# Ordering the start of a convolution-attention kernel by a list schedule, loading one image once, and projecting d and u onto repeated columns

## The chip, the cores and the metric

The kernel runs on one core of a Trainium2 chip. The metric is the device time of one execution in microseconds (us). Every time named here comes from an execution that fell in the fast state, except that single runs of a kernel have the state "unknown", which is said where it matters. Two sessions of the same kernel differ by 1 to 2 us; so a time is compared with the kernel before from the same rounds.

## The reference, cut to what matters

A tensor of four images, 64 x 64 tokens of 96 channels, goes through two layers. In the first, each image is normalised by groups and by tokens and projected to 288 + 3 x 1536 columns. A linear recurrence over the 4096 tokens with 16 states a channel follows:

```python
xn = (x - mu) * jax.lax.rsqrt(var + EPS) * ln_gamma + ln_beta
proj = xn.reshape(B, L, C) @ W_in + b_in
value, gate, delta = proj[..., :C], jax.nn.sigmoid(proj[..., C:2*C]), proj[..., 2*C:3*C]   # u, g, d
# A, Bm, Cm: the other 3 * C * S columns, S = 16
def step(h, ins):
    A_t, B_t, C_t, d_t, u_t, g_t = ins
    d = d_t[..., None]
    h_new = d * (A_t * h) + d * (B_t * u_t[..., None])
    y = g_t * jnp.sum(C_t * h_new, axis=-1)
    return (h_new, y)
# x = x + scan(...) @ W_out + b_out; then linear attention and a feed-forward block with rounding to 8 bits
```

## The kernel before: the parts that the change and the argument touch

The work is cut into 32 chunks of 512 tokens (eight for each image), and each chunk into twelve tiles of 128 partitions, which are 32 channels times 4 of the 16 states. A loop over 384 steps has one tile's scan on VectorE in each step; B and A are projected three and one steps ahead, and the small work of other chunks is hung on steps. Before the loop a straight sequence prepares chunk 0. A float32 product is computed as three products of split operands: `xs` holds 96 high rows and 32 low rows, `xl` the other low rows twice.

```python
    for i in range(NCH):
        load_gx(0, i, "x")            # image 0 in wide rows, for the group statistics alone
    ...
    load_x(0, 0)                      # and again in the order of the chunks
    raw0 = load_raw("cha", 0, A0)
    raws = [load_raw("chb", B0, C * S)]
    load_x(0, 1)
    raws += [load_raw("chb", c0, C * S) for c0 in (A0, C0)]
    ...
        def low(self):
            ...
            nc.vector.tensor_tensor(lo, self.ps, xs[0:C, :].bitcast(F32), ALU.subtract)
            nc.sync.dma_start(xl[0:64, :].bitcast(F32), lo[0:64, :].bitcast(F32))
            nc.sync.dma_start(xl[64:P, :].bitcast(F32), lo[0:64, :].bitcast(F32))
            nc.sync.dma_start(xs[C:P, :].bitcast(F32), lo[64:C, :].bitcast(F32))
    ...
        def copy(self, k, cg, engine):        # d or u of 32 channels onto four groups of partitions

            t = rep[self.b, self.i][:, k, cg]
            for q in range(4):
                engine.dma_start(
                    t[q * 32 : (q + 1) * 32], self.dd[cg * 32 : (cg + 1) * 32, k]
                )
    ...
    first.proj(2)
    first.d_out()
    first.copy(0, 0, nc.sync)
    low(2, 0, nc.vector)
    first.proj(0)
    first.du_out()
    first.copy(1, 0, nc.scalar)
    first.proj(1)
    first.gate_out()
    low(2, 1, nc.vector)
    low(2, 2, nc.vector)
    for cg in (1, 2):
        first.copy(0, cg, nc.sync)
        first.copy(1, cg, nc.sync)
```

The loop, which stays as it is:

```python
    while s < K or any(n >= s for n in steps):
        # B of tile s+3 (TensorE, ACT), A of s+1, C of s (TensorE), u*B of s+2 (GpSimd)
        ...
        if 0 <= s < K:
            tiles[s].scan()           # VectorE
        if 0 <= s + 1 < K:
            tiles[s + 1].a_mul()      # VectorE
        if 0 <= s < K and not tiles[s].on_pool:
            tiles[s].c_mul()          # VectorE
        call(s)                       # whatever hangs on this step
```

## Time and profile before

| | before |
|---|---|
| median of the first 4 runs | 1274.65 us (1273.69 to 1275.44) |
| first scan, fourth scan (step 3) | 46.2, 57.7 us |
| scan of step 12 (second chunk) | 92.1 us |
| VectorE busy, whole run | 88% |

A row of the timeline reads: start in us, duration, engine, line of the kernel, operation, output<-inputs; in brackets the idle time of the engine just before and what ended it. `SPq` is SyncE's queue of DMA issues. A row of stretches reads: stretch, length, then for TensorE, its weight loads, VectorE (DVE), ScalarE (ACT) and GpSimd (POOL) the busy time and the number of instructions, then the granted clock of TensorE (1.00 is full speed), the busy share of the DMA engines and GB/s. The lines of the kernel before stand in the prediction below.

### The profile page before, as it was taken

The numbers are of one execution on the slowest core, as the hardware profiler recorded it, in microseconds if no ns is written. First come the engines' busy times: TensorE is split into PE (matmuls) and PEld (weight loads), VectorE is DVE, ScalarE is ACT, GpSimd is POOL, SyncE is SP. The second block draws the span as 40 slices with busy tenths as digits, with TensorE's granted clock in tenths as the row PEclk, the third lists the DMA queues.
The fourth block names the chain that finished last, engine by engine and source line by source line (L and its number), as shares of the span: only waits on it lengthen the run. The fifth ranks groups of instructions, "written<-read, shape, count | busy, mean of one in ns | idle before, by whom it ended". The sixth has DMA issues, their size and how long they took to land. (4 is left out here: it accounts for less than half of the span.)

```text
span 1273.8 us, 18972 instructions
## 1 busy us (share of the span) xinstructions
PE 1171.9 (92%) x5782; PEld 882.7 (69%) x5782; DVE 1119.6 (88%) x2082; ACT 817.0 (64%) x1825; POOL 1034.8 (81%) x1189
## 2 busy tenths in 40 slices
PE   3789999999999999889999999989999999999684
PEld 2567777777777777667777777657777777777363
DVE  5479999989999999969999999869999999999274
ACT  4355555555555687567777777656676777766664
POOL 4367888888888899869999999869999889979354
PEclk7689999999999999989999999989999999999655
DMA  8567777767777778657677887656777777765221
GB/s 202 118 139 145 159 153 159 165 145 158 154 160 162 154 164 174 141 128 156 149 171 155 170 170 159 136 117 143 167 156 170 162 154 155 157 147 106 69 57 38
DMA packets 102260, 185.99 MB, mean 146 GB/s; under 512 B 42881, under 2 KB 47429, under 8 KB 102158
## 3 DMA queue, kind: packets, MB, share of 16 engines
q1 hardware_dynamic: 87708, 109.78, 37.3%
q0 software_dynamic: 13680, 74.72, 29.6%
q8 instruction: 46, 0.75, 0.3%
q10 hardware_dynamic: 770, 0.28, 0.1%
q14 instruction: 56, 0.46, 0.1%
HBM read 70.69 MB, written 24.77 MB: 75 GB/s over the span
## 5 line engine op out<-in xcount | busy, mean ns | idle before, releaser
L604 POOL TENSOR_TENSOR bu<-bu,rep 128x512 f32<-128x512 f32 x384 | 557.3, 1499 | 44.1 <-DMA rep<-dd 21.8
L601 ACT ACTIVATE bu<-Bps,b_bac 128x512 f32<-128x512 f32 x384 | 264.2, 688 | 305.0 <-PE Bps L241 281.7
L620 DVE TENSOR_TENSOR_SCAN h<-Aps,state,bu 128x512 f32<-128x512 f32 x336 | 426.5, 1269 | 9.5 <-DVE Aps L613 0.5
L613 DVE SCALAR_TENSOR_TENSOR Aps<-Aps,b_bac,rep 128x512 f32<-128x512 f32 x384 | 282.7, 736 | 61.8 <-PE Aps L241 53.0
L241 PE MATMUL Bps<-xs,w 128*128 128x512 f32 x768 | 271.4, 435 | 7.6 <-ACT bu L601 7.5
L241 PE MATMUL Aps<-xs,w 128*128 128x512 f32 x768 | 252.2, 409 | 12.4 <-DVE h L620 11.4
L241 PE MATMUL Cps<-xs,w 128*128 128x512 f32 x768 | 244.8, 400 | 0.0
L653 POOL TENSOR_TENSOR ch<-ch,h 128x512 f32<-128x512 f32 x128 | 193.6, 1512 | 3.0 <-ACT ch L650 2.8
L644 DVE SCALAR_TENSOR_TENSOR ch<-Cps,b_bac,h 128x512 f32<-128x512 f32 x256 | 189.8, 741 | 2.8 <-PE Cps L241 2.7
L241 PEld LDWEIGHTS Aps<-xs,w 128*128 128x128 f32 x768 | 141.2, 192 | 70.3 <-DVE h L620 40.7
L241 PEld LDWEIGHTS Cps<-xs,w 128*128 128x128 f32 x768 | 146.4, 191 | 36.2
L241 PEld LDWEIGHTS Bps<-xs,w 128*128 128x128 f32 x768 | 131.9, 194 | 50.9 <-issue 26.0
L241 PE MATMUL Bps<-xl,w 128*128 128x512 f32 x384 | 154.3, 402 | 0.0
L241 PE MATMUL Aps<-xl,w 128*128 128x512 f32 x384 | 154.3, 402 | 0.0
L241 PE MATMUL Cps<-xl,w 128*128 128x512 f32 x384 | 152.7, 398 | 0.0
L659 POOL DMA_DIRECT2D ch<-ch x95 | 89.4, 942 | 25.4 <-DMA ch<-ch 20.6
L650 ACT ACTIVATE ch<-Cps,b_bac 128x512 f32<-128x512 f32 x128 | 88.0, 688 | 27.3 <-PE Cps L241 26.5
L241 PEld LDWEIGHTS Cps<-xl,w 128*128 128x128 f32 x384 | 73.1, 190 | 18.5
L241 PEld LDWEIGHTS Bps<-xl,w 128*128 128x128 f32 x384 | 73.7, 192 | 17.4
L241 PEld LDWEIGHTS Aps<-xl,w 128*128 128x128 f32 x384 | 73.0, 190 | 17.2
L241 PE MATMUL dug_ps<-xs,w_dug 128*96 128x512 f32 x192 | 62.8, 409 | 10.4 <-DMA xs<-lo 10.4
L620 DVE TENSOR_TENSOR_SCAN h<-Aps,bu 128x512 f32<-128x512 f32 x48 | 58.0, 1209 | 4.8 <-POOL bu L604 3.3
(166 smaller groups left out, 1776.2 us busy)
## 6 DMA issues: line engine op xcount, KB each, us to landing
ch<-ch POOLq DMA_DIRECT2D x95, 768.0 KB, 6.8
rep<-ddd SPq DMA_DIRECT2D x124, 384.0 KB, 7.0
ddd<-dd SPq DMA_DIRECT2D x31, 384.0 KB, 3.1
xl<-lo SPq DMA_DIRECT2D x64, 128.0 KB, 3.1
gx<-in_x_dram SPq DMA_DIRECT2D x32, 192.0 KB, 3.9
x<-in_x_dram SPq DMA_DIRECT2D x32, 192.0 KB, 3.0
xatd<-xat SPq DMA_DIRECT2D x32, 192.0 KB, 3.2
xal<-xatd SPq DMA_DIRECT2D x32, 192.0 KB, 3.1
```

Of the source, the lines that this page charges most:

```text
L241: nc.tensor.matmul(ps, lhsT=wt[:, n], rhs=mv, start=(n == 0), stop=(n == 2))
L601: nc.scalar.activation(self.bu, self.b_ps, AF.Identity, bias=self.bias(0))
L604: nc.gpsimd.tensor_tensor(self.bu, self.bu, rep[self.b, self.i][:, 1, self.cg], ALU.mult)
L613: nc.vector.scalar_tensor_tensor(self.a_ps, self.a_ps, self.bias(1), rep[self.b, self.i][:, 0, self.cg], ALU.add, ALU.mult,)
L620: nc.vector.tensor_tensor_scan(self.h, self.a_ps, self.bu, 0.0 if self.i == 0 else state[self.sh, self.cg], ALU.mult, ALU.add,)
L644: nc.vector.scalar_tensor_tensor(self.slot(), self.c_ps, self.bias(2), self.h, ALU.add, ALU.mult)
L650: nc.scalar.activation(self.ch, self.c_ps, AF.Identity, bias=self.bias(2))
L653: nc.gpsimd.tensor_tensor(self.ch, self.ch, self.h, ALU.mult)
L659: nc.gpsimd.dma_start(chs[g, 0], chs.pop((g, sh)), accum_op=ALU.add)
```

## The change

Its intent is to shorten the time until the loop runs at its pace. It has five parts: image 0 is loaded once, in the chunks' layout; d and u of chunk 0 are projected straight onto 128 partitions by weights whose columns are repeated four times, so that 24 copies go; the low rows of chunk 0 are written in place by three subtractions instead of one and three DMAs; everything up to step 3 is issued in the order of a list schedule (it picks one job after the other, that which can start first, by the author's costs and landing times); and matmuls without use ("fillers") fill TensorE's planned gaps to hold its clock. Core of the diff:

```diff
     for i in range(NCH):
-        load_gx(0, i, "x")
+        load_x(0, i)
+        gxt[0, i] = xt[0, i]
# ... the second loads of x(0, 0) and x(0, 1) and the argument "tag" go
+    def repeat(n):
+        for k, c0 in enumerate((2 * C, 0)):
+            for cg in range(NCG):
+                c = c0 + cg * 32
+                nc.gpsimd.tensor_copy(
+                    w_rep[:, n, k * NCG + cg].rearrange("p (q c) -> p q c", q=4),
+                    w_dug[:, n, c : c + 32].unsqueeze(1).to_broadcast([P, 4, 32]),
+                )
# ... weights are now copied per group of 32 channels (512 columns); the bias rows get a second set for d and u
+    class Plan:
+        HOP = 0.15
+        LOOK = 0.3
# ... job(engine, cost, fn, after=, take=, free=, late=); run() picks the job that can start first,
# ... among those within LOOK that of the lower rank, then that of the longer tail
+                e = j["engine"]
+                if fill is not None and e == "PE":
+                    for _ in range(int(max(0.0, t - self.time.get(e, t) - 0.2) / 0.3)):
+                        fill()
+                j["fn"](*j["args"])
+                j["end"] = self.time[e] = t + j["cost"]
# ... group norm: diagonal, spread and its copy in two halves for image 0; for images 1 to 3:
-        for n, name in enumerate(("moments", "mean", "root", "diagonal", "spread")):
+        for n, name in enumerate(("moments", "mean", "root", "diagonal", "spread", "spread_out")):
+        def low_in_place(self, n):
+            if n == 0:
+                split[self.b, self.i] = self.xs, sb("xl", [P, TC], F32R, f"xl_{self.nm}")
+            xs, xl = split[self.b, self.i]
+            dst, c0, c1 = ((xs[C:P], 64, C), (xl[0:64], 0, 64), (xl[64:P], 0, 64))[n]
+            nc.vector.tensor_tensor(dst, self.ps[c0:c1], xs[c0:c1].bitcast(F32), ALU.subtract)
+
+        def wide(self, k, cg):
+
+            ps = self.wd[k, cg] = bank("M", [P, TC], f"wide{k}{cg}_ps")
+            project(ps, w_rep[:, :, k * NCG + cg], split[self.b, self.i])
+
+        def wide_d(self, cg):
+            if cg == 0:
+                rep[self.b, self.i] = sb("rep", [P, 2, NCG, TC], F32, f"rep_{self.nm}")
+            nc.scalar.activation(
+                rep[self.b, self.i][:, 0, cg], self.wd[0, cg], AF.Identity,
+                bias=b_rep[:, 0, cg : cg + 1],
+            )
+
+        def wide_du(self, cg):
+            t = rep[self.b, self.i]
+            nc.vector.scalar_tensor_tensor(
+                t[:, 1, cg], self.wd[1, cg], b_rep[:, 1, cg : cg + 1], t[:, 0, cg],
+                ALU.add, ALU.mult,
+            )
# ... planned_start(): one job for each operation
+        raw = [land(f"raw{n}", t) for n, t in enumerate((13.0, 16.5, 20.0))]
+        for n in range(3):
+            a = job("DVE", 0.7, first.low_in_place, n, after=[a], free=["M:x"] if n == 2 else [])
+        d, u = [], []
+        for cg in range(NCG):
+            t = mm(0.7, first.wide, 0, cg, after=[a, w["rep"]], key=f"M:d{cg}")
+            d.append(job("ACT", 0.69, first.wide_d, cg, after=[t, b, *d[-1:]], free=[f"M:d{cg}"]))
+            t = mm(0.7, first.wide, 1, cg, after=[t], key=f"M:u{cg}")
+            u.append(job("DVE", 0.74, first.wide_du, cg, after=[t, d[-1]], free=[f"M:u{cg}"]))
# ... the tiles up to step 3; then rank 1: the second chunk
+        job("DVE", 0.7, second.low, after=[a], free=["M:x2"])
# ... the filling matmul
+            nc.tensor.matmul(
+                awake[0][:, 0:P], lhsT=ident, rhs=ident, start=True, stop=True
+            )
```

## The prediction

> **What bounds the kernel now.** I read the busy shares and the forty slices of the page, then the busy time of the engines in stretches, then the timeline of the first 95 us with its waits. The slices first (busy tenths, one digit for 31.8 us):
>
> ```profile
> PE   3789999999999999889999999989999999999684
> ...
> DVE  5479999989999999969999999869999999999274
> ```
>
> After the third slice VectorE is at nine tenths and more for nearly the whole run: about 32.4 us for each chunk of twelve tiles (twelve scans, twelve multiplications of A, eight of C, and the small work). The change touches none of that; it orders only what comes before step 3 of the loop. So its worth is read from the first slices. Busy time in stretches of the start (columns: stretch, its length, PE, weight loads, DVE, ACT, POOL, granted clock, DMA share, GB/s):
>
> ```profile
> 0.00:26.00 26.00, 9.22 (x46) 6.58 (x46) 13.11 (x35) 10.72 (x18) 12.09 (x32) 0.77 0.83 209
> 26.00:46.00 20.00, 11.69 (x29) 7.67 (x30) 7.93 (x15) 9.58 (x15) 4.20 (x5) 0.59 0.67 141
> 46.00:58.00 12.00, 8.33 (x29) 6.11 (x28) 7.52 (x10) 2.92 (x6) 5.29 (x5) 0.78 0.54 128
> 58.00:92.00 34.00, 29.16 (x115) 22.34 (x113) 22.77 (x34) 17.90 (x45) 22.87 (x22) 0.84 0.59 129
> 92.00:124.60 32.60, 31.84 (x144) 23.81 (x143) 32.15 (x54) 17.65 (x44) 25.76 (x28) 1.00 0.67 137
> ```
>
> From 26 to 46 us no engine is busy for even 60%. Something is waited for there, and the waits say what (timeline of GpSimd, then of VectorE and TensorE; start, duration, instruction, idle before it and what ended that):
>
> ```profile
> 41.80 1.27 POOL L604 TENSOR_TENSOR bu<-bu,rep 128x512 f32<-128x512 f32 x1 [12.12 <-DMA rep<-dd]
> 47.65 1.29 POOL L604 TENSOR_TENSOR bu<-bu,rep 128x512 f32<-128x512 f32 x1 [4.58 <-DMA rep<-dd]
> 54.00 3.72 POOL L604 TENSOR_TENSOR bu<-bu,rep 128x512 f32<-128x512 f32 x3 [5.06 <-DMA rep<-dd]
> ```
> ```profile
> 46.21 1.21 DVE L620 TENSOR_TENSOR_SCAN h<-Aps,bu 128x512 f32<-128x512 f32 x1
> ...
> 57.74 1.21 DVE L620 TENSOR_TENSOR_SCAN h<-Aps,bu 128x512 f32<-128x512 f32 x1
> 61.48 0.76 DVE L613 SCALAR_TENSOR_TENSOR Aps<-Aps,b_bac,rep 128x512 f32<-128x512 f32 x1 [2.53 <-PE Aps L241]
> ```
> ```profile
> 56.44 1.17 PE L241 MATMUL dug_ps<-xs,w_dug 128*96 128x512 f32 x2 [3.67 <-DMA xs<-lo]
> ```
>
> GpSimd waits 21.8 us in three waits for the copies of d and u, which are 24 DMAs of 64 KB; SyncE issues them at about 0.6 us each (16 in 13.75 us). The first scan begins at 46.21, the fourth (step 3) at 57.74. The same SyncE queue holds back the transfers of the second chunk's low rows, so that TensorE stands until 56.44. These two times, 57.74 and 56.44, are what the change has to move.
>
> **What the Trainium skill says.** "TensorE: Matmul & The Clock Gate", What's actually happening: after an idle window of some 3.4 us the array falls to half rate and needs about as long of work to come back. The trace agrees: the granted clock is 0.50 from 15 to 30 us, and a matmul of 512 columns takes about 0.43 us there against 0.235 after 48 us. "DMA: Bandwidth & Descriptors", Specifications: the line rate needs 512 bytes or more. The trace agrees: while loads of x in rows of 384 bytes ran alone (522 packets at 12.5 to 14.5 us), most slices showed 115 to 200 GB/s; the 1,536-byte loads of gx ran at 279 from 2 to 6 us. "SBUF — State Buffer", SBUF: two separate sides: VectorE with two SBUF inputs and GpSimd lock each other out. The trace is consistent: the power of 128x4 took 1.65 us beside the weight subtractions and 1.04 us at 67.9 us.
>
> **The change part by part.**
>
> *x once.* The eight gx loads (3.5 us to landing, rows of 1,536 bytes) become x loads with rows of 384 bytes. At 165 to 190 GB/s (estimate from the slices above) 0.197 MB takes 1.03 to 1.2 us, eight take 8.3 to 9.5 us against about 7. From the first bytes at 1.9 us the last lands near 10.9 instead of 9.3: +1.6 us on the statistics. Two separate x loads (2.2 us of DMA) go, so the weights land when they did.
>
> *Chain to the first projection*, before: last group statistics end 10.7, normalised z 22.65, low rows 25.58, after three DMAs TensorE starts at 28.86. After, with the same rows of the trace: statistics end 12.3; aggregate, mean and root 3.15 (10.72 to 13.83, as before) gives 15.45; diagonal 0.4, spread of half the columns 0.7 instead of 1.1, copy 0.3: 16.9. Centre now ran earlier, scale 0.56: 17.5. Statistics 1.03, offset 0.1, power 1.05 to 1.65 (say 1.35): 20.0 (the other three GpSimd operations, 1.3 us, leave the path). Apply on VectorE 1.7 (four took 1.69 at 1247 us), last transpose 0.4, affine 0.73, upper 0.58, hops: 23.7. Low rows in place, three subtractions of 0.69: 25.8. TensorE starts there, 3 us earlier; the subtractions cost 1.4 us more of VectorE but no DMA (3.3 us).
>
> *d and u by repeated columns.* Out: d_out, which stood behind three weight casts until 34.11, and 24 copies until 52. In: six projections onto 128 rows instead of two onto 96, 18 matmuls at 0.235 = 4.2 us of TensorE (7.7 if the clock stays low), three ACT copies of 0.69, three VectorE multiplications of 0.74 instead of one. Two GpSimd repetitions (2 x 2.2 us by the author's own figure) and 0.4 MB of DMA lie beside the chain. First multiplication of B: 25.8 + 0.7 + 0.7 + 0.75 = 28.0; with 1.3 us on GpSimd the first scan starts at **29.5 against 46.21: 16.7 us** earlier.
>
> *The list schedule* then has to fit all the rest. VectorE after 25.8: du 3 x 0.74, A 4 x 0.75, scans 3 x 1.22, C 2 x 0.75, about four of the nine weight subtractions at 1.0 (the raw weights land too late for more), second chunk 1.1 + 0.7 = 16.2 us. So step 3 can't start before **42**, 15.7 us earlier. TensorE: 6 + 6 + 4 + 3 projections of 0.7 = 13.3 us, to 39, if the filling matmuls hold the clock. So the 16.7 us are partly lost again: VectorE takes the place of the DMA.
>
> *The second chunk* has rank 1, so its statistics, power 1.8, apply 1.55, transpose 0.5, affine and upper 1.3, low 0.7 fill holes. With VectorE full they come late, I think low rows at 40 to 43. Its three DMAs (3.3 us) follow, and the next matmul in TensorE's order is proj 2 of that chunk: TensorE resumes at 43 to 46 against 56.44, **10.5 to 13.5 us** earlier, and probably at half clock again.
>
> *After step 3* nothing is different: the 4.66 us wait for gx at 80 us and the slow tiles (34 us for nine, against 24 in the steady state) stay.
>
> The sum: between 10.5 and 15.7 us, and I choose 13: 1274.3 - 13.3 = **1261 us**, or 1.0%.
>
> **The rivals.** (1) *VectorE is the only bound and the second chunk gets in early*: then step 3 counts and some of the ten lost microseconds between 58 and 92 go too, since they began with that wait; 17 to 22 us, 1252 to 1257. For it: ACT and GpSimd have room. (2) *Late data in a fixed order*: queues are strict, the plan assumes x at 3.6 + 0.8n and weights at 13.0, 16.5 and 20.0; before, the x rows were slower than that. A cast that waits for its weights ahead of the spread's copy on ACT delays everything by 1 to 3 us, and the clock falls to half if the filling is too thin (up to 12 us of TensorE): only 4 to 8 us, 1266 to 1270. (3) *The start is hidden anyway*: if some later DMA set the pace, nothing would come of it; against it, VectorE is at 97% of the stretch from 92 us on, so an earlier start is an earlier end.
>
> **Range and chances.** The rivals' ends give 1252 to 1269. Faster by over 2% needs 25.5 us, more than the first scan itself gains, so 0.04. Slower by 2% would need a new stall of 39 us in the start: 0.01.
>
> **What would show each step.** First scan near 29.5 and fourth near 42 to 44; no DMA rep<-dd; last x landing near 11; first wide projection near 26; waits of 3 us for xs<-lo in TensorE around 43; granted clock near 1.0 from 26 to 40; the scan that opens the second chunk at about 79 instead of 92.06; the end of the run shifted by the same amount. The prediction is wrong if step 3 starts before 36 (the weight subtractions fitted in earlier), if the wait for xs<-lo is gone, or if the gap between the fourth scan and the second chunk shrinks below 30 us.

## The result, and the profile after

The changed kernel takes **1259.96 us** (median of 4 runs, 1258.66 to 1262.39), before 1274.65. The ratio is **0.9887** with a 95% interval of 0.9869 to 0.9906, so 1.1% less. A ratio is the mean time of one kernel's fast runs over that of the other's of the same rounds, so not quite the ratio of the medians. The prediction said 1261. But the traces show that its sum came out right from parts that did not.

The slices of the changed kernel's page, to be laid beside those of before:

```profile
PE   7989999999999999799999999889999999999683
...
DVE  6779999999999999779999999869999999999275
```

The first two slices are fuller (VectorE 6 and 7 against 5 and 4); from the fourth on they differ by a tenth here and there. The same stretches as in the prediction, now of the changed kernel:

```profile
0.00:26.00 26.00, 18.19 (x107) 16.14 (x107) 14.27 (x35) 9.93 (x15) 14.55 (x41) 0.87 0.83 204
26.00:46.00 20.00, 18.48 (x93) 14.59 (x94) 19.01 (x32) 12.85 (x23) 10.48 (x10) 1.00 0.37 86
46.00:58.00 12.00, 9.42 (x38) 7.00 (x37) 5.36 (x7) 4.68 (x11) 8.29 (x7) 0.86 0.36 90
58.00:92.00 34.00, 28.99 (x116) 21.66 (x115) 26.36 (x38) 17.58 (x45) 22.59 (x22) 0.90 0.71 155
```

From 26 to 46 us VectorE is now busy 19.0 of 20 us, where it was busy 7.9: the wait for DMA has become a full engine. After 46 us it is idle for more than half again. The timeline of the same trace says what each part came to:

```profile
15.75 1.07 ACT L278 CAST w<-raw 128x512 fp32r<-128x512 f32 x1 [2.51 <-DMA raw<-in_L_conv_W_in_dram]
19.43 0.24 ACT L557 COPY gmr<-gmr_ps 128x96 f32<-128x96 f32 x1 [2.61 <-PE gmr_ps L548]
...
35.39 3.25 POOL L742 TENSOR_TENSOR bu<-bu,rep 128x512 f32<-128x512 f32 x2 [5.72 <-DVE rep L666]
...
37.70 1.22 DVE L758 TENSOR_TENSOR_SCAN h<-Aps,bu 128x512 f32<-128x512 f32 x1
```

GpSimd's wait for the copies (12.1 us before) is a wait of 5.7 us for VectorE, and the first scan begins at 37.7 instead of 46.2. It would have been earlier, had the spread of the group statistics not waited for TensorE until 19.4. TensorE's timeline shows why, and what stands at step 4:

```profile
13.98 5.04 PE L1141 MATMUL awake<-ident 128*128 128x128 f32 x22
18.81 0.58 PE L548 MATMUL gmr_ps<-gdg,ones 96*128 96x96 f32 x2
...
48.97 0.70 PE L245 MATMUL dug_ps<-xs,w_dug 128*96 128x512 f32 x2 [2.37 <-DMA xs<-lo]
```

The 11 filling matmuls (listed as 22 instructions, 0.23 us each at half clock) stand in the queue ahead of the spread, whose operand was ready at 13.25. And TensorE still waits for the second chunk's low rows, until 48.97 instead of 56.44. VectorE pays for it (its timeline):

```profile
47.30 1.22 DVE L758 TENSOR_TENSOR_SCAN h<-Aps,bu 128x512 f32<-128x512 f32 x1
53.70 0.76 DVE L751 SCALAR_TENSOR_TENSOR Aps<-Aps,b_bac,rep 128x512 f32<-128x512 f32 x1 [5.18 <-PE Aps L245]
54.56 1.22 DVE L758 TENSOR_TENSOR_SCAN h<-Aps,bu 128x512 f32<-128x512 f32 x1
```

So the gain is 8.5 us at the first scan, 10.4 at the fourth, 7.8 at the fifth and 8.2 at step 12 (83.9). The end of this trace is 13.1 us earlier. Some 5 us came where the change seemed to do nothing.

### The profile page after: what moved, and what is told of

The parts are those of the page before. It is cut to its first block, busy times and chain, and to the rows that moved or that the text cites. A ratio compares the mean times of both kernels' runs of the same rounds, so it can differ in the third digit from the quotient of the medians.

```text
span 1260.7 us, 19196 instructions
## 1 busy us (share of the span) xinstructions
PE 1175.9 (93%) x5885; PEld 890.3 (71%) x5885; DVE 1124.9 (89%) x2093; ACT 818.4 (65%) x1824; POOL 1038.9 (82%) x1198
## 5 line engine op out<-in xcount | busy, mean ns | idle before, releaser
L758 DVE TENSOR_TENSOR_SCAN h<-Aps,state,bu 128x512 f32<-128x512 f32 x336 | 426.7, 1270 | 9.2
L245 PE MATMUL dug_ps<-xs,w_dug 128*96 128x512 f32 x188 | 59.4, 397 | 2.4 <-DMA xs<-lo 2.4
L768 ACT COPY state<-h 128x1 f32<-128x1 f32 x336 | 61.0, 181 | 0.0
```

The source lines that it names most:

```text
L245: nc.tensor.matmul(ps, lhsT=wt[:, n], rhs=mv, start=(n == 0), stop=(n == 2))
L758: nc.vector.tensor_tensor_scan(self.h, self.a_ps, self.bu, 0.0 if self.i == 0 else state[self.sh, self.cg], ALU.mult, ALU.add,)
L768: nc.scalar.copy(st, self.h[:, TC - 1 : TC])
```

## The experiments

Twelve runs followed: nine altered kernels, the changed kernel once more and the kernel before twice. All results were correct. Scans are numbered from 0: s0 is the first, s12 opens the second chunk, s383 is the last. Each timeline number is of one trace; "end" is from s383 to the end of the trace.

| run | median us | ratio to before (95%) | s0 | s3 | s4 | s12 | s12 to s383 | end |
|---|---|---|---|---|---|---|---|---|
| before, first trace | 1274.65 | 1 | 46.2 | 57.7 | 62.4 | 92.1 | 1085.2 | 96.5 |
| before, second trace | 1273.49, one run | | 47.1 | 58.3 | 62.5 | 91.8 | 1084.8 | 95.2 |
| before, third trace | 1268.05, one run | | 46.8 | 58.1 | 62.0 | 90.8 | 1084.5 | 91.0 |
| changed, first trace | 1259.96 | 0.9887 (0.9869-0.9906) | 37.7 | 47.3 | 54.6 | 83.9 | 1082.0 | 94.8 |
| changed, again | 1259.24 | 0.9889 (0.9867-0.9910) | 37.0 | 46.7 | 53.9 | 83.1 | 1079.0 | 94.5 |
| no fillers ahead of the spread | 1258.06 | 0.9881 (0.9858-0.9905) | 35.0 | 44.6 | 50.3 | 79.1 | 1081.3 | 94.9 |
| no fillers at all | 1257.98 | 0.9894 (0.9874-0.9913) | 36.3 | 45.8 | 51.6 | 80.5 | 1081.2 | 95.2 |
| x twice | 1258.05 | 0.9892 (0.9873-0.9912) | 36.6 | 46.2 | 52.8 | 81.4 | 1080.6 | 94.7 |
| low rows by DMA | 1256.39 | 0.9875 (0.9853-0.9897) | 37.1 | 47.0 | 49.7 | 78.6 | 1081.5 | 96.0 |
| copies of d and u | 1268.08 | 0.9963 (0.9952-0.9974) | 39.5 | 58.5 | 61.2 | 89.6 | 1081.3 | 94.9 |
| second chunk in place | 1251.85 | 0.9841 (0.9815-0.9868) | 37.4 | 47.4 | 49.9 | 77.9 | 1081.5 | 90.2 |
| third piece at step 14 | 1253.55 | 0.9851 (0.9827-0.9876) | 36.9 | 46.5 | 52.1 | 74.0 | 1081.6 | 94.8 |
| three edits together | 1250.01 | 0.9820 (0.9793-0.9847) | 35.3 | 45.3 | 47.9 | 69.7 | 1082.3 | 95.5 |
| spread and copy in one step | 1260.55 | 0.9912 (0.9886-0.9937) | 36.0 | 45.6 | 52.4 | 81.1 | 1081.4 | 95.0 |

My theory after the first trace was that the start sets the end, by way of three waits: the fillers, the second chunk's DMA, and a later load that the change leaves alone. The rival was that VectorE, now full, makes these waits worthless.

**The changed kernel again** (no edit).

> The changed kernel once more, unaltered. In its first trace the opening scan of the second chunk (step 12) lay only 8.2 us earlier than before (83.9 against 92.1), while the end lay 13.1 us earlier; the other 5 us appeared at four places far behind the change. Theory 'start only': those 5 us are chance of the two traces, step 12 is again near 84, and the stretch from step 12 to the last scan differs from the first trace's 1082.0 us by up to 2 us. Rival 'something later is better as well': the stretch is again about 1082 us, and 3 us shorter than before's 1085.2 us in every trace.

Step 12 is again near 83, but the stretch after it is 1079.0: neither branch quite, and 3 us between two traces of one program. It is taken up below.

**No fillers ahead of the spread.**

```diff
-                if fill is not None and e == "PE":
+                if fill is not None and e == "PE" and j["fn"].__name__ != "spread":
```

> The 11 filling matmuls ahead of the first spread are left out, the other 32 stay. Theory 'fillers hold the chain': in the changed kernel they run from 14.0 to 19.0 us on TensorE, the spread behind them in the queue starts at 18.8 although its operand was there at 13.3. Without them the first spread is done by 14.5; its copy on ACT then stands behind the first weight cast, which ends at 16.8, so the copy moves from 19.4 to 16.9 and the first scan from 37.7 to 35.2 (2.5 us earlier), the end by 1 to 2.5 us. Rival 'fillers pay': the clock falls lower (it is 0.5 there anyway) and the first projections run at half rate; no gain or a loss of 1 to 3 us.

The timeline of ACT in this run, then of its VectorE:

```profile
14.60 1.06 ACT L278 CAST w<-raw 128x512 fp32r<-128x512 f32 x1 [1.70 <-DMA raw<-in_L_conv_W_in_dram]
15.56 0.23 ACT L557 COPY gmr<-gmr_ps 128x96 f32<-128x96 f32 x1
```
```profile
16.63 1.82 DVE L596 TENSOR_TENSOR z<-x,gmr 128x384 f32<-128x384 f32 x1
18.37 1.76 DVE L235 TENSOR_TENSOR w<-raw,w 128x512 fp32r<-128x512 f32 x1
20.05 0.55 DVE L599 TENSOR_TENSOR z<-z,gmr 128x384 f32<-128x384 f32 x1
```

As expected, the copy now stands behind the weight cast, at 15.56 instead of 19.43, and the first scan is at 35.0, 2.0 to 2.7 us earlier than in the two traces of the changed kernel. Step 12 is 4 to 5 us earlier. The time moved by 1.2 to 1.9 us (medians), inside the intervals: the hold is shown, its worth at the end is not resolved. The lines of VectorE show what holds the chain next: the copy of the second half ends at 17.15 (near the predicted 16.9), but the scale ends at 20.60, because a long centring and a weight subtraction stand before it in VectorE's queue.

**No fillers at all.**

```diff
-        plan.run(stay_awake)
+        plan.run()
```

> No filling matmul at all (43 are left out). Theory 'the later fillers pay': the spread is early as in the run without the first eleven, but the clock is 0.5 until some 5 us after the first projection, projections take 1.28 instead of 0.70 us; first scan 37 to 38.5 instead of 35.0, the end 1 to 3 us later than with the later 32. Rival 'the clock is irrelevant here, VectorE sets the pace': first scan 35 to 36 and the same time as that run.

Stretches of this run, then of the run before it, which keeps 33 fillers (the column after GpSimd's is the granted clock):

```profile
20.00:30.00 10.00, 3.09 (x8) 1.81 (x9) 9.72 (x32) 8.16 (x12) 4.70 (x5) 0.50 0.82 193
30.00:40.00 10.00, 10.00 (x39) 7.97 (x38) 9.04 (x11) 4.22 (x7) 4.12 (x3) 0.85 0.41 94
```
```profile
20.00:30.00 10.00, 8.65 (x61) 7.59 (x61) 9.82 (x33) 7.91 (x12) 4.74 (x5) 0.95 0.74 182
30.00:40.00 10.00, 9.98 (x46) 7.72 (x45) 9.69 (x13) 4.86 (x10) 5.04 (x4) 1.00 0.40 93
```

(The traces of the changed kernel list 88 filling instructions, two for each filler: 44 fillers, and 33 without the first 11. The expectations count one less.) The 33 later fillers do hold the clock, 0.95 against 0.50, and that is worth 1.3 us at the first scan and 1.4 at step 12, less than expected. These are single traces, and two traces of the changed kernel differ there by 0.7 and 0.8. At the end nothing is seen (1257.98 and 1258.06). All 44 together cost at the first scan more than they brought: it comes at 36.3 without them, at 37.0 and 37.7 with them. At the end that is not resolved (ratios 0.9894 and 0.9889).

**x loaded twice**: the loads of before were put back.

> One part undone: image 0 is loaded twice again, eight times in wide rows for the statistics, and x of each chunk by itself. Theory 'loading once is worth nothing here': last statistics end near 10.7 instead of 11.7, but the weights land about 2 us later; the first spread is held by the fillers to 19 anyway; first scan 37 to 39, the end the same within 1.5 us. Rival 'the saved loads pay later': the six x loads that return to the first chunks delay the other transfers there, the stretch from step 12 to the last scan grows from 1079-1082 towards the 1085 of before.

Loading once is worth nothing that shows: 1258.05 against 1259.24, with step 12 1.7 us earlier. The stretch after step 12 is 1080.6, so the rival is out.

**Low rows of chunk 0 by DMA again.**

```diff
-        for n in range(3):
-            a = job("DVE", 0.7, first.low_in_place, n, after=[a], free=["M:x"] if n == 2 else [])
+            if n == 0:
+                a = job("DVE", 0.7, first.low, after=[a], free=["M:x"], late=3.3)
```

(The `for` line stays in the source; only its first turn now does anything.)

> One part undone: the low rows of the first chunk go by one subtraction and three DMAs again, as before the change. Theory 'in place saves the transfer': three subtractions took 2.1 us on VectorE, one and a transfer of 3.3 us take 4.0; first scan at 39 instead of 37.0, step 12 at 84.5 to 85 instead of 83.1, the end later by 1 to 2 us. Rival 'VectorE is the bound in this stretch': it gets 1.4 us back, so the fourth scan stays near 46.7 and the time is the same.

The theory missed: s0 did not move. The rival's numbers hold (s3 at 47.0, the time inside the intervals), but neither foresaw that s4 came 4 to 5 us **earlier**. The second chunk explains it. Its low rows on VectorE, and the issue of their DMA, in this run's timeline:

```profile
32.33 0.69 DVE L623 TENSOR_TENSOR lo<-xnt_ps,xs 96x512 fp32r<-96x512 f32 x1
...
36.76 0.55 SPq L624 DMA_DIRECT2D xl<-lo  x1
```

The same two in the changed kernel:

```profile
44.75 0.68 DVE L623 TENSOR_TENSOR lo<-xnt_ps,xs 96x512 fp32r<-96x512 f32 x1
...
45.46 0.46 SPq L624 DMA_DIRECT2D xl<-lo  x1
```

The order of issue has changed. My reading, which no run shows by itself: while the engines wait for the transfer, the list schedule has a hole, and the second chunk, which has the lower rank, is put into it; in place, the hole closed and the second chunk was pushed back by 12 us. TensorE waits 0.8 us for the first chunk's xs<-lo here and not at all for the second chunk's.

**Second chunk's low rows in place as well.**

```diff
-        job("DVE", 0.7, second.low, after=[a], free=["M:x2"])
+        for n in range(3):
+            a = job("DVE", 0.7, second.low_in_place, n, after=[a], free=["M:x2"] if n == 2 else [])
```

> The low rows of the second chunk too are written in place by three subtractions on VectorE, without the three DMAs. Theory 'the second chunk's DMA sets step 4': TensorE stood 2.4 us until 48.97 for them, its clock fell to half, and the fifth scan was at 54.6; now TensorE goes on at about 47 with its clock at full, the fifth scan comes at 50 to 51, and the end moves by 3 to 4 us. Rival 'VectorE is the bound there': it gets 1.4 us more work, the fifth scan moves by 1 us or less and the time is the same.

The timeline of TensorE and VectorE in this run:

```profile
46.73 0.16 PEld L245 LDWEIGHTS dug_ps<-xl,w_dug 128*96 128x96 f32 x1 [0.43 <-DVE xl L649]
...
49.07 0.76 DVE L751 SCALAR_TENSOR_TENSOR Aps<-Aps,b_bac,rep 128x512 f32<-128x512 f32 x1 [0.49 <-PE Aps L245]
...
49.94 1.22 DVE L758 TENSOR_TENSOR_SCAN h<-Aps,bu 128x512 f32<-128x512 f32 x1
```

The wait of 2.4 us is 0.4, VectorE's of 5.2 is 0.5, and s4 is at 49.9 as expected. The medians moved by 7.4 us, the means of the runs (1259.2 and 1253.2) by 6.0; s4 and s12 by 4 to 6. The trace has an end of 90.2 besides, which is taken up below. The wait for the second chunk's DMA is the one that set step 4.

**Third piece of image 1 summed at step 14.**

```diff
-            when[0:2] = 4, 7
+            when[0:3] = 4, 7, 14
```

> Only the step at which the third piece of image 1 is summed is moved from 8 to 14, its load still issued at step 7. Theory 'untouched stall': before and after the change TensorE waits 4.7 us for that load (at 75.3 before, 67.3 after), VectorE 5.8 us, so a start earlier by 8 us simply meets the same wait 8 us earlier; without it the scan of step 12 moves from 84 to about 78.5 and the end by 4 to 6 us. Rival 'the wait is replaced': the copies of d and u of the second chunk or the gather land at the same time and are needed next, the gain is under 2 us.

The wait in the changed kernel and its VectorE before the eleventh scan (s10), then this run's VectorE before the same scan:

```profile
PE gx_ps L475 <- DMA gx<-in_x_dram: 4.7, 1, 4.7
```
```profile
68.73 1.22 DVE L758 TENSOR_TENSOR_SCAN h<-Aps,bu 128x512 f32<-128x512 f32 x1
75.72 0.76 DVE L751 SCALAR_TENSOR_TENSOR Aps<-Aps,b_bac,rep 128x512 f32<-128x512 f32 x1 [5.77 <-PE Aps L245]
```
```profile
66.30 1.21 DVE L758 TENSOR_TENSOR_SCAN h<-Aps,bu 128x512 f32<-128x512 f32 x1
67.43 0.73 DVE L751 SCALAR_TENSOR_TENSOR Aps<-Aps,b_bac,rep 128x512 f32<-128x512 f32 x1
...
68.73 1.21 DVE L758 TENSOR_TENSOR_SCAN h<-Aps,bu 128x512 f32<-128x512 f32 x1
```

In the changed kernel 7.0 us pass from the start of one scan to the multiplication for the next (68.7 to 75.7), here 1.1. Step 12 is 9 us earlier (some of it already at s4, which varies), and 1.8 us are given back by scan 60 (s16 and s17 together take 1.8 us more here than in the other traces, and 1.6 more in the run with three edits). The medians moved by 5.7 us, as expected, the means by 4.7.

**Copies of d and u instead of repeated columns** (with these go the repeated weights, GpSimd's work on them and their transfers; all else is kept):

```diff
-        for cg in range(NCG):
-            t = mm(0.7, first.wide, 0, cg, after=[a, w["rep"]], key=f"M:d{cg}")
-            ...
+        t = mm(0.7, first.proj, 2, after=[a, wd], key="M:pd")
+        dj = job("ACT", 0.68, first.d_out, after=[t, b], free=["M:pd"])
+        t = mm(0.7, first.proj, 0, after=[dj], key="M:pu")
+        uj = job("DVE", 0.75, first.du_out, after=[t, dj], free=["M:pu"])
+        for cg in range(NCG):
+            d.append(job("SP", 2.4, first.copy, 0, cg, nc.sync, after=[dj], late=2.0))
+            ...                        # u likewise, its first group on ACT's queue
```

> One part undone: d and u of chunk 0 are again projected once and copied to four groups of partitions by 24 DMAs of 64 KB, with the list schedule, the low rows in place and x once kept. Theory 'the repeated columns are the heart': d is out at 33.3, the copies' issues take 0.6 us each, the first scan comes at 40 to 42, the third near 50 (41.7 with columns), the fourth near 53 (46.7), the end is 4 to 7 us later. Rival 'step 4 hides it': the fifth scan waits for the second chunk anyway (53.9); then it moves by 2 us or less and the end too.

The timeline of this run:

```profile
31.46 14.46 SPq L647 DMA_DIRECT2D rep<-dd  x20
...
44.90 2.51 POOL L749 TENSOR_TENSOR bu<-bu,rep 128x512 f32<-128x512 f32 x2 [1.62 <-DMA rep<-dd]
...
52.39 1.22 DVE L765 TENSOR_TENSOR_SCAN h<-Aps,bu 128x512 f32<-128x512 f32 x1
```

SyncE issues 20 copies in 14.5 us, the third scan comes at 52.4 (41.7 to 42.3 with columns), and the time is 1268.1: 8.8 us more than the changed kernel of the other session, and more than the 4 to 7 expected. Only 2.0 us at step 12 are left against the mean of before (91.6). So of the 8.1 us that the start gains, about 6 are the repeated columns. The third and fourth scan are later than the theory said; the rival (2 us or less) is out.

**Where the other microseconds came from.** The kernel before was traced twice more, one run each (state unknown).

> The kernel before, unaltered, traced again: its one trace so far took 1085.2 us from the scan of step 12 to the last scan and 96.5 us from there to the end, all nine traces with changed starts 1079.0 to 1082.0 and 90.2 to 96.0. Theory 'chance of one trace': a new trace shows about 1081 and 95, step 12 near 92 as before, and a total of about 1268. Rival 'the start changes what follows': 1085 and 96.5 again, total 1274.

> The same once more, for the same question: two traces tell a lasting difference in the stretch after step 12 from a draw between two outcomes (of 27 runs of this kernel the lowest took 1267.6 us, the highest 1276.8).

Two things come apart here. From s12 to s383 the three traces of before take 1084.5 to 1085.2, eleven traces with changed starts 1079.0 to 1082.3 (mean 1081.2). The ranges do not touch: the rival holds, and 3 to 4 us are a lasting difference in a loop whose work is the same. The end, in contrast, is a draw. Stretches of the second and of the third trace of before:

```profile
1220.00:1230.00 10.00, 8.64 (x45) 7.03 (x44) 6.90 (x29) 5.25 (x9) 6.29 (x12) 0.57 0.24 61
```
```profile
1220.00:1230.00 10.00, 7.41 (x65) 5.55 (x64) 9.74 (x44) 8.31 (x12) 7.58 (x15) 1.00 0.33 88
```

The same program gets through 65 matmuls instead of 45 where the clock was granted in full, and its end takes 91.0 us instead of 95.2; the run with the second chunk in place drew the same luck (90.2). This may be why the 27 runs of before of one session lie between 1267.6 and 1276.8; it is shown for two traces only.

**Spread and its copy in one step for images 1 to 3.** The prediction had overlooked that the change also moves this copy one step later, and 1.5 to 2 of the lost microseconds lie just there.

```diff
-        for n, name in enumerate(("moments", "mean", "root", "diagonal", "spread", "spread_out")):
+        for n, name in enumerate(("moments", "mean", "root", "diagonal", "both")):
```

> The one part of the change that acts after step 3, overlooked in the prediction, undone: for images 1 to 3 the copy of the spread group statistics on ACT is again issued in the same step as its matmul, not one step later. Three traces of the kernel before take 18.4 to 18.5 us from scan 264 to scan 268 (the group statistics of image 3 fall there), ten traces with changed starts 16.4 to 17.1. Theory 'this copy is the cause': 18.4 us again, and the stretch from step 12 to the last scan grows from about 1081.3 to 1082.8 or more; the time is 1 to 2 us longer. Rival 'the cause is elsewhere': 16.4 to 17.1 and 1079 to 1082, no change in time.

(The numbers in this expectation add the intervals that end at scans 265, 267 and 268; the one at 266 is 2.1 us in every trace. In the ten traces the sum is 16.3 to 17.5.) They came to 17.0, the stretch to 1081.4, the time to 1260.55: the rival. This copy is not the cause.

**Three edits together**: no fillers ahead of the spread, the second chunk in place, the third piece at step 14.

> Three edits together on the changed kernel: no fillers ahead of the first spread, low rows of the second chunk in place, third piece of image 1 summed at step 14. Theory 'they act one after the other': first scan 35, fifth 47 to 48, step 12 at 69 to 70 instead of 83, then the stretch of 1081.6 and the end of 95 as in the single runs; the time 1246 to 1249 us, against before 2% or a little more. Rival 'VectorE is full by then': the sum of the single gains is not reached, step 12 at 73 to 74, 1252 us.

s0 at 35.3, s4 at 47.9 and step 12 at 69.7 are as the theory of waits one after the other says. The time is 1250.01 us (1243.3 to 1252.4), just above the expected range, a ratio of 0.9820. Both kernels are beaten: before clearly, and the changed kernel by its ratio from another session (0.9889, 0.9867 to 0.9910), with intervals that do not touch. Whether it is 2% below before stays unclear by its interval. Of the 13.8 us gained at step 12 over the changed kernel (83.5, mean of two traces), 9.2 reach the median.

## Why the prediction was right or wrong

- **The time, 1261 us and "within 2%", was right** (1259.96), by luck, as the parts below show. The bound was right as well: GpSimd's wait for the copies and TensorE's for the second chunk were what had to move, and the busy time of VectorE from 26 to 46 us rose to 95%, as rival and main line both had it.
- **"Chain to the first projection" failed by about 6 us.** It put the spread's copy at 16.9 and the low rows at 25.8; they ended at 21.06 and 31.47. The term left out is the 11 fillers: they were in the diff, and the prediction counted them only as a way to hold the clock, not as entries in a queue. They account for nearly all of the copy's 4.2 us: without them it ended at 17.15, although a weight cast stood before it (rival 2). That gave 2.0 to 2.7 us back at the first scan. The rest is VectorE's queue, which the prediction's chain passed without waiting: the scale ended 5.8 us late, since a weight subtraction held it until 22.0 and it then took 1.33 us beside GpSimd's like operation instead of 0.56. In the run without the 11 fillers it was still 3.1 us late for the same kind of reason.
- **From the low rows to the first scan, 3.7 us were predicted, 6.2 passed**: the projection of B was put ahead of that of d, and weight subtractions ahead of the first du. So the first scan was 8 us later than the 29.5 predicted. VectorE's work from the low rows to step 3 was sized well: 16.2 us predicted, 15.8 passed (31.47 to 47.30).
- **Step 3 at 42 was 46.7 to 47.3; TensorE's resumption at 43 to 46 was 48.97; step 12 at 79 was 83.1 to 83.9.** Each shift was right in kind and mis-sized: 13 us predicted at step 12, 8.1 measured (91.6 and 83.5, means of three and two traces).
- **That a wait for xs<-lo remains at TensorE was right** (2.4 us; 3 were predicted), and the in-place run showed that it sets step 4. The prediction took its lateness for a matter of a full VectorE. The run with low rows by DMA showed that its low rows can come 12 us earlier; that the schedule gives the second chunk only the holes is my reading.
- **"After step 3 nothing is different" failed in the other direction.** The 4.7 us wait for gx stayed, as said, and the run without it was 5.7 us faster (4.7 by the means). But the stretch after step 12 lost 4.3 us (1084.8 to 1080.5, means of three and two traces). This is what brought the wrong parts to the right sum: 8.1 and 4.3 are 12.4 of the 14.7 us between the first medians; the rest is no more than the traces draw in the end.
- **x loaded once**: its last landing was predicted near 11 and TensorE's last wait for x ended at 10.36; its rate was mis-sized (239 GB/s from 2 to 6 us, 165 to 190 predicted). It is worth nothing that shows; the prediction had even charged 1.6 us for it.
- **Its signs of being wrong did not appear**: step 3 did not start before 36, the wait for xs<-lo was there, and the gap from step 3 to step 12 was 36.6 us, not under 30. The clock was 1.00 from 26 to 40, as said. Three small slips changed nothing: 16 issues in 13.75 us are 0.86 us each (their median is 0.59), the sum of 13 is subtracted as 13.3, and the rivals' ends reach 1270, not 1269.

**What stays open** is the cause of those 3 to 4 us. It is not the double load, not the columns, not the in-place rows, not the fillers and not the later copy: each was undone alone and the stretch stayed at 1080.6 to 1081.5 (two of them that each suffice are not excluded). What all eleven traces share and before lacks is the list schedule, with what came along in the same diff: the copies of weights by groups, the small loads in another order, the group statistics of image 0 in two halves. In all of them the interval to scan 112 is 2.0 to 2.2 us, against 2.4 to 3.3 in the three traces of before, where TensorE waits 0.2 to 1.2 us for the transfer xs<-lo. Part of that wait is SyncE's: in these three traces it issues the first of the chunk's three transfers 0.39 us after VectorE's subtraction ends, in the eleven others 0.06 to 0.08. Why it does, no run says. One rival is untested: a start with other instructions shifts everything in the queues, the packets that fetch instructions included (102 in the first trace of before). Nor is it shown that a gain at step 12 always arrives whole at the end: the traces draw 3 us in the stretch and 6 in the end.

## What to carry to other kernels

A list schedule is no better than its picture of the queues: an instruction that fills a gap on paper is an obstacle in an in-order queue as soon as the real times slip, so put fillers only behind the last thing that the critical chain needs from that engine. Work of low rank lives in the holes of a plan; when you close a hole, look where that work went and what waits for it. And check a right total by its parts, at marks along the run: here a start that gained 5 us less than predicted and a loop that gained 4 us unpredicted added up to the forecast.

## What the Trainium skill lacked or had wrong

- "TensorE: Matmul & The Clock Gate", Why this matters for your kernels, says to leave no idle gaps of more than some 3 us between bursts of matmuls, so that the clock stays up. It lacks the price of filling them: a float32 filler of 128 x 128 took 0.46 us at half clock and 0.23 at full, 11 of them held a ready matmul from 13.98 to 18.81 us, and the 33 later ones brought 1.3 us at the first scan.
- The same page, What's actually happening, calls the windows of the clock gate free-running and the warm-up different from run to run at its start. It lacks that the clock can differ between runs late in a kernel too: from 1220 to 1230 us it was 0.57 in one trace of the same program and 1.00 in another, whose end was 4.2 us shorter. That the windows are the reason, no run shows.
- "DMA: Bandwidth & Descriptors", Specifications, puts the line rate at 512 bytes and more, and has no figure there for shorter rows. Here rows of 384 bytes, with little else in flight from 2 to 6 us, ran at 239 GB/s against 279 for rows of 1,536 bytes: 14% less.
- For the time that SyncE needs to issue one DMA, "DMA: Bandwidth & Descriptors" has only a count of cycles for "previous generations"; I know of no page with a measured time on this chip. In the run with copies one issue of 64 KB took 0.51 to 0.81 us (median 0.59), and 20 took 14.46. Each landed 2.0 to 2.1 us after its issue, so there the issues, and not the bytes, spaced the copies.
